# Beginning the second attention inside the local layers' last steps, and preparing batch 1 of the first attention beside the first maxima

## Chip, cores and metric

One core of a Trainium2 chip runs the whole program. The time is the device time of one execution in microseconds (us); lower is better. The engines are PE (matrix products), DVE (vector), ACT (scalar, activation functions), POOL (general, slower elementwise work) and SP (it issues most transfers). PSUM is the accumulator memory that PE writes, SBUF the working memory.

## The reference

The program is a chain of four blocks on `x` of 2 batches x 1024 tokens x 128 features, all in float32. Each block is followed by the sum with its own input and a layer norm.

```python
x = _layernorm(x + _L0_attn_ref(x, ...))   # 16 heads of 8, softmax over the keys, all 1024 keys
x = _layernorm(x + _L0_ffn_ref(x, ...))    # 2 local layers: windowed attention (window 64, 8 heads
                                           # of 64, rotary, l2 norm), then a gated GELU feed-forward
x = _layernorm(x + _L1_attn_ref(x, ...))   # causal attention, 2 query heads of 128, one key/value head
x = _layernorm(x + _L1_ffn_ref(x, ...))    # 8 experts, 2 chosen for each token
```

The first and the third are called first and second attention below.

## The kernel before

The order of the instructions is written out by hand. Every stage is a loop over steps, a function such as `project(n)` issues its instructions on several engines when it is called, and each engine runs its own in the order of the calls. Dictionaries (`also`, `early`, `late`, ...) hold further calls for certain steps: `at(late, 35, f)` means that `f` is called at the end of step 35. `late` comes last in a step.

**First attention** (`first_attention`, L136). It works in 16 units `m` (batch, group of four heads, half of the queries), units 0 to 7 for batch 0, 8 to 15 for batch 1. A unit takes 16 steps. In each step PE makes two score tiles of 128 x 512 (`max_score`, L226) whose maxima DVE takes (L232), and, `LATE` = 21 steps later, two transposed score tiles (`exp_score`, L258) that ACT exponentiates (L263) and PE multiplies with the values (L270). So steps 0 to 20 have only score tiles and maxima. At the end of each unit DVE combines its maxima (`max_row`, L236), PE turns the row, and ACT copies it out of PSUM (`max_shift`, L245). All PSUM tiles of this stage come from one ring of 8 (`ring`). Before the loop batch 0 is prepared: `prepare_x` transposes `x` (L88) and copies it to SBUF (L174), `project` makes keys and queries (L180, copies L182 and L184), `prepare_values` makes the values (L209, copy L213). Batch 1 is prepared by the same functions inside the loop: the six calls in `prepares` at steps 84, 86, ... 94, `prepare_values` at steps 132 and 134. Unit 8, at step 128, is the first that needs them; the transfers that spread its keys and queries over the partitions are issued at step 108.

**Local layers** (`local_layers`, L562). 32 tiles of 128 tokens go through a pipeline in steps 2 to 37; tile `n` is projected in step `n` and leaves in step `n + 6` (`add_x`), so that the last steps hold fewer and fewer functions. After every four tiles a feed-forward block follows (`ff_shift`, `ff_stats`, `ff_norm`, `ff_turn`, three chunks of `ff_in` and `ff_gate`, `ff_out`, `ff_add`). Of the last two blocks, (layer 1, batch 0, half 1) starts in step 33 and ends in step 37; (1, 1, 1) can start only when tile 31 has left and is computed in the second attention. The PSUM tiles are `double` (1024 wide, three) and `single` (512 wide, two). `last_sum` adds the block's input and prepares its norm.

**Second attention** (`second_attention`, L952). 16 tiles go through steps 0 to 20 (`one`). In step `n` tile `n` is projected (`project`, L970) and rotated (`rotate`: two products on DVE L983, a copy of the values on ACT L987, two sums on POOL L989 and L990); in step `n + 1` it is transposed (`transpose_qk`: PE L88, ACT L998 and L1001); in step `n + 2` come `scores` (L1012) and `exps` (DVE L1025 and L1026, ACT L1027). Its input comes from `head(b, hf)`: four transposes and an ACT copy (L963) for half a batch. Heads (0,0) and (1,0) are made before step 0. The last feed-forward block (1,1,1) is interleaved with steps 0 to 5, the norm of half (0,1) stands in step 1 and the norm of half (1,1) in step 6. `scores` and `ff_in` share the two `double` tiles of this stage's own PSUM pool `psc`.

The expert stage follows from step 16 on. Its loads, lookups and scatters are not touched.

Of the kernel before, what the change touches and what calls it, by code (L numbers as in the profile page):

```python
# [7 lines left out]
F32 = mybir.dt.float32  # L8
# [4 lines left out]
P = 128  # L13
B = 2
T = 1024
D = 128
# [31 lines left out]
def transformer_kernel(ctx: ExitStack, tc: tile.TileContext, a, out):  # L48
# [87 lines left out]
    def first_attention(pool, pool2, poolf, brief, psm, loads, experts, ws, tab, begin):  # L136
# [27 lines left out]
        def prepare_x(b, hf):  # L164
            if hf == 0:
                xTs[b] = pool2.tile([P, T], F32, tag="xT", name=f"xT{b}", bufs=1)
                zs[b] = poolf.tile([P, 8, D], F32, tag="z", name=f"z{b}", bufs=1)
                alls[b] = [
                    brief.tile([P, T], F32, tag=f"all{n}", name=f"all{n}{b}") for n in range(2)
                ]  # L170
            ps = ring("ps_xT")
            transpose_tiles(ps, lambda i: x[b, hf][:, i, :], 4)
            part = xTs[b][:, hf * 512 : (hf + 1) * 512]
            (nc.vector.tensor_copy if hf else nc.scalar.copy)(part, ps)  # L174

        def project(b, hf, n):

            ps = ring("ps_qk")
            part = slice(hf * 512, (hf + 1) * 512)
            nc.tensor.matmul(ps, wa[:, n, :], xTs[b][:, part], start=True, stop=True)  # L180
            if n == 0:
                nc.scalar.activation(alls[b][n][:, part], ps, AF.Copy, scale=8.0 ** -0.5)  # L182
            else:
                nc.vector.tensor_copy(alls[b][n][:, part], ps)  # L184

        def spread_k(u):

# [17 lines left out]
        def prepare_values(b, hf):  # L205
            ps = ring("ps_v")
            for i in range(4):
                t = hf * 4 + i
                nc.tensor.matmul(  # L209
                    ps[:, i * P : (i + 1) * P], xTs[b][:, t * P : (t + 1) * P], wa[:, 2, :],  # L210
                    start=True, stop=True,
                )
            nc.vector.tensor_copy(  # L213
                vps[b][:, hf * 4 : hf * 4 + 4, :, 0:8].rearrange("p t h d -> p (t h) d"),
                ps.rearrange("p (n d) -> p n d", d=8),
            )
# [123 lines left out]
        def at(step, f, *args):  # L340
            also.setdefault(step, []).append((f, args))
# [3 lines left out]
        for u in range(1, UNITS // 2):  # L345
            at(32 * u - 20, spread_q, u, 0, nc.sync)
            at(32 * u - 20, spread_k, u)
            at(32 * u - 20, spread_q, u, 1, nc.sync)
            for hf in range(2):
                at(32 * u - 4 + 2 * hf, keep_q, 2 * u + hf)  # L350
        for i, (f, *args) in enumerate(prepares):
            at(16 * 8 - 44 + 2 * i, f, 1, *args)
        for hf in range(2):
            at(16 * 8 + 4 + 2 * hf, prepare_values, 1, hf)
        for m in range(UNITS):
            at(16 * m + 15, max_row, m)
            at(16 * m + 16, max_shift, m)
# [204 lines left out]
    def local_layers(ws, tab):  # L562
# [282 lines left out]
            x_at[layer, b, hf] = x[b, hf]  # L845
            head(layer, b, hf)

        def steps(p, p2, ps, finish):
            nonlocal pool, pool2, psl
            pool, pool2, psl = p, p2, ps  # L850

# [59 lines left out]
            at(turns, 6, head, 0, 0, 1)  # L911
            at(turns, 10, head, 0, 1, 1)

            def run(f, n, *args):
                if 0 <= n < N:
                    f(n, *args)
# [32 lines left out]

    def second_attention(pool, pool2, poolf, single, double, route, wc, woc, cs, ws, left):  # L952
        N = 16
        tiles = [(b, t) for t in range(8) for b in range(B)]
        kTs = {b: pool.tile([P, T], F32, name=f"kTc{b}") for b in range(B)}
        vs = {b: pool.tile([P, 8, D], F32, name=f"vc{b}") for b in range(B)}
        xTs, ys, st = {}, {}, [{} for _ in range(N)]

        def head(b, hf):
            ps = single("ps_xTc")  # L960
            transpose_tiles(ps, lambda i: x[b, hf][:, i, :], NT)
            xTs[b, hf] = pool2.tile([P, 512], F32, tag="xTc", name="xTc", bufs=4)
            nc.scalar.copy(xTs[b, hf], ps)  # L963
            ys[b, hf] = pool2.tile([P, NT, D], F32, tag="yc", name=f"yc{b}{hf}", bufs=4)

        def project(n):
# [7 lines left out]
        def rotate(n):  # L974
            b, t = tiles[n]
            s = st[n]
            ps = s.pop("ps")

            q4 = ps[:, :384].rearrange("p (n d) -> p n d", d=64)
            t1 = pool2.tile([P, 3, 2, 64], F32, tag="t1c", name="t1c", bufs=2)  # L980
            t2 = pool2.tile([P, 3, 2, 64], F32, tag="t2c", name="t2c", bufs=2)
# [6 lines left out]
            rot = s["rot"] = pool2.tile([P, 3, 2, 64], F32, tag="rotc", name="rotc", bufs=2)  # L988
            nc.gpsimd.tensor_sub(rot[:, :, 0, :], t1[:, :, 0, :], t2[:, :, 1, :])  # L989
            nc.gpsimd.tensor_add(rot[:, :, 1, :], t1[:, :, 1, :], t2[:, :, 0, :])  # L990

        def transpose_qk(n):
            b, t = tiles[n]
            s = st[n]
            ps = single("ps_rotc")
            transpose_tiles(ps, lambda k: s["rot"][:, k].rearrange("p s d -> p (s d)"), 3)
            s["qT"] = pool2.tile([P, 2, P], F32, tag="qTc", name="qTc", bufs=3)
# [88 lines left out]
        def group(f, g, *args):  # L1086
            if 0 <= g < SOON:
                f(g, *args)


        norm_before, x_in, x1s, lasts = left
        ff_shift, ff_stats, ff_norm, ff_turn, ff_in, ff_gate, ff_out, ff_add = feed_forward(
            poolf, single, double, ws, x1s, lasts, mbufs=2, gbufs=4
        )
        early, late, normed = {}, {}, {}

        def at(when, step, f, *args):
# [2 lines left out]
        def do(when, step):  # L1100
            for f, args in when.pop(step, ()):
                f(*args)

        def sum_up(b):
            normed[b] = last_sum(x_in, b, 1)

        block = (1, 1, 1)
        at(late, 0, ff_shift, *block)
        at(late, 0, ff_stats, *block)
        at(early, 1, norm_before)  # L1110
        at(early, 1, ff_norm, *block)
        at(late, 1, ff_turn, *block)
        at(late, 1, head, 0, 1)
        for c, step in enumerate((2, 2, 3)):
            at(late, step, ff_in, *block, c)
            at(early, step + 1, ff_gate, *block, c)
        at(late, 4, ff_out, *block)
        at(early, 5, ff_add, *block)
        at(late, 5, sum_up, 1)
        at(early, 6, lambda: normed[1]())  # L1120
        at(late, 6, head, 1, 1)
        at(late, 1, route.lay_out)

        for b in range(B):
            head(b, 0)

        def one(step, run_experts):

# [46 lines left out]
                group(route.choose, p // 2)  # L1175
            do(late, step)

        def rest(run_experts):
            for step in range(FF_STEPS, N + 5):
                one(step, run_experts)  # L1180

        FF_STEPS = 8
        for step in range(FF_STEPS):
            one(step, None)
        assert not early and not late
        return rest

# [422 lines left out]
    ordered = {mybir.EngineType.PE, mybir.EngineType.Activation, mybir.EngineType.DVE}  # L1610
    engines = ordered | {mybir.EngineType.Pool}
    begin, steps = local_layers(ws, tab)
    with tc.tile_pool(name="af", bufs=1) as pf:


        brief = tc.tile_pool(name="a0", bufs=1, side="right")
        first = tc.tile_pool(name="l0", reuse_waits="tile", bufs=1, side="right")
        pb = brief.__enter__()

        def at_first():  # L1620
            brief.__exit__(None, None, None)
            return first.__enter__()

        with (
            tc.tile_pool(name="a1", bufs=1) as p1, tc.tile_pool(name="a2", bufs=2) as p2,
# [6 lines left out]
        with (  # L1632
            tc.tile_pool(name="l1", reuse_waits="tile", bufs=1) as p1,
            tc.tile_pool(name="l2", reuse_waits="tile", bufs=1) as p2,
            tc.tile_pool(name="psl", reuse_waits="tile", bufs=1, space=bass.MemoryType.PSUM) as psl,
            tc.manual_schedule(engines=engines),
        ):
            left = steps(p1, p2, psl, finish)
        first.__exit__(None, None, None)
    wlocal.__exit__(None, None, None)  # L1640
    with (
        tc.tile_pool(name="c1", reuse_waits="tile", bufs=1) as p1,
# [9 lines left out]

        route = Route(p1, p2, single, gate, xs)
        with tc.tile_pool(name="cf", reuse_waits="tile", bufs=1) as pf:
            rest = second_attention(p1, p2, pf, single, double, route, wc, woc, cs, ws, left)
        with tc.tile_pool(name="ce", reuse_waits="tile", bufs=1) as pe:
            run_experts = experts(pe, p2, single, double, route, ew, xs, yr)
            rest(run_experts)
            run_experts(4)


def _constants():
# [88 lines left out]
```

## Time and profile before

| what | value |
|---|---|
| median of 3 runs | 1090.54 us (1090.28 to 1091.72) |
| the profiled execution | 1090.38 us |
| its span, first to last instruction | 1088.6 us |
| busy: PE, DVE, ACT, POOL | 994.9, 802.0, 743.9, 569.3 us |
| granted PE clock, mean | 0.963 |
| first maxima (L226) to last exponent scores (L258) | 12.9 to 437.0 us |
| local layers up to the last `ff_out` (L528) | to about 830 us |
| second attention, first `project` to last `project` (L970) | 831.2 to 939.9 us |
| expert products (L1462) | 981.7 to 1062.8 us |

The span counts from the first to the last instruction; the execution's own time lies 1.8 us above it. A busy share is a mean over stages with different limits, so each stage is read from its own rows: a timeline row gives start, duration, engine, line, operation, output and inputs, count, and in brackets how long the engine had been idle and what ended that. For PE a count is of hardware passes, two for each float32 product.

### The profile page before, as it was taken

Reading aid. Unit: us, or ns where it says so; the run is one execution under the profiler, and the core shown is the slowest. Engines: PE = TensorE matmul, PEld = TensorE weight load, DVE = VectorE, ACT = ScalarE, POOL = GpSimd, SP = SyncE. Lnnn points to the kernel's source line nnn. Section 1 sums busy time; section 2 is a strip of 40 time slices with the busy share of each in tenths; the row PEclk is TensorE's granted clock in tenths of the full one; section 3 lists DMA queues with packets and bytes.
Section 4 is the critical chain, followed back from the end, with each engine's and each line's share of the span. In section 5 each row is a group of like instructions: output and inputs, shape, how many; then the busy total and the mean of one; then the engine's idle time right before and its main releaser. Section 6 shows DMA issues by size and latency. Waiting matters only on the chain. (4 is left out here: it accounts for less than half of the span.)

```text
span 1088.6 us, 21891 instructions
## 1 busy us (share of the span) xinstructions
PE 994.9 (91%) x8091; PEld 589.4 (54%) x8091; DVE 802.0 (74%) x1681; ACT 743.9 (68%) x1503; POOL 569.3 (52%) x625
## 2 busy tenths in 40 slices
PE   8999999999999999779889999999787799999991
PEld 4533333333333332356666657676564466689891
DVE  6988878888898886868969678696754387757443
ACT  1488878888888887568878788797763555444442
POOL 4134333434543433678978686786732135408753
PEclk9799999999999999989999999999898899999996
DMA  3111523122220200200101001010000000146883
GB/s 91 33 38 50 147 60 87 42 59 59 60 55 13 79 2 1 74 21 21 31 21 26 21 17 31 21 31 21 16 2 1 0 1 23 42 158 206 307 302 125
DMA packets 57210, 65.09 MB, mean 60 GB/s; under 512 B 9076, under 2 KB 43424, under 8 KB 57104
## 3 DMA queue, kind: packets, MB, share of 16 engines
q1 hardware_dynamic: 53472, 57.40, 17.9%
q0 software_dynamic: 2272, 4.92, 1.3%
q8 instruction: 64, 1.05, 0.4%
q10 hardware_dynamic: 1360, 1.38, 0.4%
q14 instruction: 42, 0.34, 0.1%
HBM read 37.98 MB, written 19.67 MB: 53 GB/s over the span
## 5 line engine op out<-in xcount | busy, mean ns | idle before, releaser
L232 DVE TENSOR_REDUCE mx<-s_max 128x1 f32<-128x512 f32 x512 | 318.2, 684 | 57.1 <-PE s_max L226 52.3
L263 ACT ACTIVATE pr<-s_exp 128x512 f32<-128x512 f32 x512 | 265.6, 602 | 71.1 <-PE s_max L226 58.7
L226 PE MATMUL s_max<-kTb,qm 32*128 32x512 f32 x1024 | 262.9, 642 | 0.5 <-DMA qm<-all 0.5
L282 POOL TENSOR_TENSOR av<-av,avp 128x512 f32<-128x512 f32 x101 | 128.0, 1267 | 245.7 <-ACT avp L281 226.6
L258 PE MATMUL s_exp<-q,kTb 32*128 32x512 f32 x1024 | 253.1, 616 | 0.0
L258 PEld LDWEIGHTS s_exp<-q,kTb 32*128 32x128 f32 x1024 | 101.2, 184 | 88.1 <-DVE mx L232 66.8
L270 PE MATMUL av<-pr,vp 128*32 128x512 f32 x1024 | 137.2, 605 | 0.7 <-ACT pr L263 0.7
L226 PEld LDWEIGHTS s_max<-kTb,qm 32*128 32x128 f32 x1024 | 113.6, 190 | 36.1 <-ACT pr L263 13.5
L755 ACT ACTIVATE pm<-pm,nb,rn 128x128 f32<-128x128 f32 x256 | 105.5, 490 | 0.1
L657 POOL TENSOR_TENSOR t<-raw,tab 128x512 f32<-128x512 f32 x64 | 87.1, 1381 | 19.4 <-DVE raw L625 10.8
L690 POOL TENSOR_TENSOR rn<-rn,neghalf 128x16 f32<-128x16 f32 x32 | 94.0, 2937 | 2.7
L649 DVE TENSOR_TENSOR t<-raw,tab 128x1024 f32<-128x1024 f32 x32 | 40.8, 1273 | 54.7 <-ACT raw L642 54.5
L270 PEld LDWEIGHTS av<-pr,vp 128*32 128x32 f32 x1024 | 20.5, 108 | 98.4 <-ACT pr L263 94.5
L636 PE MATMUL ps_qk<-wqkv,hT 128*128 128x512 f32 x120 | 58.8, 613 | 3.0 <-DVE o L788 2.5
L281 ACT COPY avp<-av 128x512 f32<-128x512 f32 x101 | 60.0, 594 | 1.8 <-PE av L270 0.6
L499 PE MATMUL ps_w<-hnT,w 128*128 128x512 f32 (+1 forms) x96 | 48.3, 635 | 13.1 <-DVE mt L517 9.8
L642 ACT COPY raw<-ps_qk 128x512 f32<-128x512 f32 x60 | 32.2, 589 | 38.1 <-PE ps_qk L636 37.4
L689 POOL TENSOR_SCALAR rn<-rn 128x16 f32<-128x16 f32 x32 | 31.1, 970 | 46.1 <-DVE rn L688 45.6
L1467 ACT ACTIVATE gj<-ps_fc 128x512 f32<-128x512 f32 x39 | 23.3, 597 | 41.2 <-PE ps_fc L1462 39.9
L1482 POOL DMA_INDIRECT yr<-yj,to x39 | 37.4, 958 | 23.1 <-DVE yj L1478 19.3
L688 DVE TENSOR_REDUCE rn<-sq 128x16 f32<-128x1024 f32 x32 | 38.6, 1208 | 9.5 <-ACT sq L664 9.4
L731 PEld LDWEIGHTS ps_sim<-kT,qT 64*64 64x64 f32 x1024 | 28.3, 135 | 31.9 <-issue 15.1
(230 smaller groups left out, 2012.1 us busy)
## 6 DMA issues: line engine op xcount, KB each, us to landing
wj<-ew SPq DMA_DIRECT2D x39, 512.0 KB
xs<-zero SPq DMA_DIRECT2D x8, 1152.0 KB
vh<-vb SPq DMA_DIRECT2D x60, 130.0 KB
xj<-xs SPq DMA_DIRECT2D x39, 72.0 KB
tab<-in_tab SPq DMA_DIRECT2D x2, 1024.0 KB
ew<-in_proj_w SPq DMA_DIRECT2D x8, 256.0 KB
ew<-in_fc_w SPq DMA_DIRECT2D x1, 2048.0 KB
wqkv<-in_wqkv SPq DMA_DIRECT2D x2, 768.0 KB
```

Of the source, the lines that this page charges most:

```text
L226: nc.tensor.matmul(s, q[32 * head : 32 * head + 32, qt * P : (qt + 1) * P], k[32 * head : 32 * head + 32, kh * 512 : (kh + 1) * 512], star ...
L232: return lambda: nc.vector.reduce_max(mx[:, head, qt, kh : kh + 1], s, axis=AX.X)
L258: nc.tensor.matmul(s, k[32 * head : 32 * head + 32, kt * P : (kt + 1) * P], q[32 * head : 32 * head + 32, :], start=True, stop=True,)
L263: return lambda: nc.scalar.activation(pr[:, head, :], s, AF.Exp)
L270: nc.tensor.matmul(ps[32 * h : 32 * h + 32, :], vps[m // 8][:, kt, 4 * g + h, :], pr[:, h, :], start=True, stop=True,)
L281: nc.scalar.copy(part, ps)
L282: nc.gpsimd.tensor_add(avs[m], avs[m], part)
L499: nc.tensor.matmul(ps[:m, n * 512 : (n + 1) * 512], w["w1"][:, n * HID + c0 : n * HID + c0 + m], f["hnT"], start=True, stop=True,)
L636: nc.tensor.matmul(ps[:, k * 512 : (k + 1) * 512], s["hT"], w["wqkv"][:, k * 512 : (k + 1) * 512], start=True, stop=True,)
L657: nc.gpsimd.tensor_mul(s["t2"][:, :, :, lo : lo + 32], raw4[:, :, :, hi : hi + 32], tabls[layer][:, t, 1, :, lo : lo + 32].unsqueeze(2).to ...
L690: nc.gpsimd.tensor_tensor(rn, rn, neghalf.to_broadcast([P, 16]), ALU.pow)
L755: nc.scalar.activation(s["pm"][:, k, :], s["pm"][:, k, :], AF.Exp, scale=s["rn"][:, head : head + 1], bias=s["nb"][:, k : k + 1],)
```

## The change

The change has two independent parts.

**Batch 1 of the first attention.** The six calls of `prepares` move from steps 84 to 94 to steps 1, 3, ... 11, and the two calls of `prepare_values` from 132 and 134 to 13 and 17. All their copies out of PSUM go to ACT for batch 1 (before, one of the two of `prepare_x`, both of the keys and both of the values were DVE's). The tiles `all0` and `all1` that hold queries and keys get a second buffer, so that batch 1 need not wait for batch 0's to be read.

**Second attention.** Heads (0,0) and (1,0), both of `project(0)`, `rotate(0)` and `project(1)`, `rotate(1)`, and `transpose_qk(0)` are called at the end of the local layers' steps 35, 36 and 37. They use the local layers' `double` PSUM tiles (their first 512 columns) and a new SBUF pool `c0` that takes the place of the pool `l0`. The second attention's loop then starts at step 2. The feed-forward block (1,1,1) and what hangs on it stand one step later than before: `ff_shift` and `ff_stats` ahead of step 2, `ff_norm` and `ff_turn` in step 2, `ff_in` in steps 3, 3 and 4, `ff_out` in 5, `ff_add` and the sum in 6, the norm and head (1,1) in 7.

```diff
-                    brief.tile([P, T], F32, tag=f"all{n}", name=f"all{n}{b}") for n in range(2)
+                    brief.tile([P, T], F32, tag=f"all{n}", name=f"all{n}{b}", bufs=2) for n in range(2)
...
-            (nc.vector.tensor_copy if hf else nc.scalar.copy)(part, ps)
+            (nc.vector.tensor_copy if hf and b == 0 else nc.scalar.copy)(part, ps)
...
-                nc.vector.tensor_copy(alls[b][n][:, part], ps)
+                (nc.scalar.copy if b else nc.vector.tensor_copy)(alls[b][n][:, part], ps)
...
-            nc.vector.tensor_copy(
+            (nc.scalar.copy if b else nc.vector.tensor_copy)(
                 vps[b][:, hf * 4 : hf * 4 + 4, :, 0:8].rearrange("p t h d -> p (t h) d"),
...
         for i, (f, *args) in enumerate(prepares):
-            at(16 * 8 - 44 + 2 * i, f, 1, *args)
+            at(1 + 2 * i, f, 1, *args)
         for hf in range(2):
-            at(16 * 8 + 4 + 2 * hf, prepare_values, 1, hf)
+            at(13 + 4 * hf, prepare_values, 1, hf)
...
+            for step, f, *args in after(double):
+                at(late, step, f, *args)
...
-        block = (1, 1, 1)
-        at(late, 0, ff_shift, *block)
-        at(late, 0, ff_stats, *block)
-        at(early, 1, norm_before)
-        at(early, 1, ff_norm, *block)
-        at(late, 1, ff_turn, *block)
-        at(late, 1, head, 0, 1)
-        for c, step in enumerate((2, 2, 3)):
-            at(late, step, ff_in, *block, c)
-            at(early, step + 1, ff_gate, *block, c)
-        at(late, 4, ff_out, *block)
-        at(early, 5, ff_add, *block)
-        at(late, 5, sum_up, 1)
-        at(early, 6, lambda: normed[1]())
-        at(late, 6, head, 1, 1)
...
-        for b in range(B):
-            head(b, 0)
...
+        def begin(p0, bank):
...
+            def enter():
+                nonlocal pool0, single
+                pool0, single = p0(), bank
+                for b in range(B):
+                    kTs[b] = pool0.tile([P, T], F32, name=f"kTc{b}")
+                    vs[b] = pool0.tile([P, 8, D], F32, name=f"vc{b}")
+                for b in range(B):
+                    head(b, 0)
+
+            def tile(n):
+                project(n)
+                rotate(n)
+
+            return [(35, enter), (36, tile, 0), (37, tile, 1), (37, transpose_qk, 0)]
...
+            block = (1, 1, 1)
+            ff_shift(*block)
+            ff_stats(*block)
+            at(early, 2, norm_before)
+            at(early, 2, ff_norm, *block)
+            at(late, 2, ff_turn, *block)
+            at(late, 2, head_too, 0, 1)
+            for c, step in enumerate((3, 3, 4)):
+                at(late, step, ff_in, *block, c)
+                at(early, step + 1, ff_gate, *block, c)
+            at(late, 5, ff_out, *block)
+            at(early, 6, ff_add, *block)
+            at(late, 6, sum_up, 1)
+            at(early, 7, lambda: normed[1]())
+            at(late, 7, head_too, 1, 1)
...
+            for step in range(2, FF_STEPS):
+                one(step, None)
...
+            left = steps(
+                p1, p2, psl, finish,
+                lambda double: begin2(at_second, lambda name: double(name)[:, :512]),
+            )
```

More of the change, by code (lines that the diff above doesn't have):

```diff
@@ L846, in next_head, with steps @@
             head(layer, b, hf)
-        def steps(p, p2, ps, finish):
+        def steps(p, p2, ps, finish, after):
             nonlocal pool, pool2, psl
@@ L946, in local_layers, with second_attention @@
         return begin, steps
-    def second_attention(pool, pool2, poolf, single, double, route, wc, woc, cs, ws, left):
+    def second_attention(wc, woc, cs, ws):
+        pool0 = pool2 = single = double = route = None
         N = 16
         tiles = [(b, t) for t in range(8) for b in range(B)]
-        kTs = {b: pool.tile([P, T], F32, name=f"kTc{b}") for b in range(B)}
-        vs = {b: pool.tile([P, 8, D], F32, name=f"vc{b}") for b in range(B)}
-        xTs, ys, st = {}, {}, [{} for _ in range(N)]
+        kTs, vs, xTs, ys, st = {}, {}, {}, {}, [{} for _ in range(N)]
         def head(b, hf):
@@ L961, in head, with make_y @@
             transpose_tiles(ps, lambda i: x[b, hf][:, i, :], NT)
-            xTs[b, hf] = pool2.tile([P, 512], F32, tag="xTc", name="xTc", bufs=4)
+            xTs[b, hf] = pool0.tile([P, 512], F32, tag="xTc", name="xTc", bufs=4)
             nc.scalar.copy(xTs[b, hf], ps)
+        def make_y(b, hf):
             ys[b, hf] = pool2.tile([P, NT, D], F32, tag="yc", name=f"yc{b}{hf}", bufs=4)
@@ L979, in rotate @@
             q4 = ps[:, :384].rearrange("p (n d) -> p n d", d=64)
-            t1 = pool2.tile([P, 3, 2, 64], F32, tag="t1c", name="t1c", bufs=2)
-            t2 = pool2.tile([P, 3, 2, 64], F32, tag="t2c", name="t2c", bufs=2)
+            t1 = pool0.tile([P, 3, 2, 64], F32, tag="t1c", name="t1c", bufs=2)
+            t2 = pool0.tile([P, 3, 2, 64], F32, tag="t2c", name="t2c", bufs=2)
             for k, o in enumerate((t1, t2)):
@@ L987, in rotate @@
             nc.scalar.copy(vs[b][:, t, :], ps[:, 384:512])
-            rot = s["rot"] = pool2.tile([P, 3, 2, 64], F32, tag="rotc", name="rotc", bufs=2)
+            rot = s["rot"] = pool0.tile([P, 3, 2, 64], F32, tag="rotc", name="rotc", bufs=2)
             nc.gpsimd.tensor_sub(rot[:, :, 0, :], t1[:, :, 0, :], t2[:, :, 1, :])
@@ L996, in transpose_qk @@
             transpose_tiles(ps, lambda k: s["rot"][:, k].rearrange("p s d -> p (s d)"), 3)
-            s["qT"] = pool2.tile([P, 2, P], F32, tag="qTc", name="qTc", bufs=3)
+            s["qT"] = pool0.tile([P, 2, P], F32, tag="qTc", name="qTc", bufs=3)
             nc.scalar.activation(
@@ L1088, in group @@
                 f(g, *args)
[L1091 to L1094, printed above, removed]
         early, late, normed = {}, {}, {}
@@ L1102, in do @@
                 f(*args)
-        def sum_up(b):
-            normed[b] = last_sum(x_in, b, 1)
-        block = (1, 1, 1)
-        at(late, 0, ff_shift, *block)
-        at(late, 0, ff_stats, *block)
-        at(early, 1, norm_before)
-        at(early, 1, ff_norm, *block)
-        at(late, 1, ff_turn, *block)
-        at(late, 1, head, 0, 1)
-        for c, step in enumerate((2, 2, 3)):
-            at(late, step, ff_in, *block, c)
-            at(early, step + 1, ff_gate, *block, c)
-        at(late, 4, ff_out, *block)
-        at(early, 5, ff_add, *block)
-        at(late, 5, sum_up, 1)
-        at(early, 6, lambda: normed[1]())
-        at(late, 6, head, 1, 1)
-        at(late, 1, route.lay_out)
-        for b in range(B):
-            head(b, 0)
         def one(step, run_experts):
@@ L1176, in one @@
             do(late, step)
+        FF_STEPS = 8
         def rest(run_experts):
@@ L1180, in rest, with steps, sum_up, head_too @@
                 one(step, run_experts)
[L1182 to L1186, printed above, removed]
+        def begin(p0, bank):
+            nonlocal pool0, single
+            def enter():
+                nonlocal pool0, single
+                pool0, single = p0(), bank
[8 more added lines that the diff above has]
+            return [(35, enter), (36, tile, 0), (37, tile, 1), (37, transpose_qk, 0)]
+        def steps(p2, poolf, sgl, dbl, rt, left):
+            nonlocal pool2, single, double, route
+            pool2, single, double, route = p2, sgl, dbl, rt
+            norm_before, x_in, x1s, lasts = left
+            ff_shift, ff_stats, ff_norm, ff_turn, ff_in, ff_gate, ff_out, ff_add = feed_forward(
+                poolf, single, double, ws, x1s, lasts, mbufs=2, gbufs=4
+            )
+            def sum_up(b):
+                normed[b] = last_sum(x_in, b, 1)
+            def head_too(b, hf):
+                head(b, hf)
+                make_y(b, hf)
+            block = (1, 1, 1)
[13 more added lines that the diff above has]
+            at(late, 7, head_too, 1, 1)
+            at(late, 2, route.lay_out)
+            for b in range(B):
+                make_y(b, 0)
+            for step in range(2, FF_STEPS):
+                one(step, None)
+            assert not early and not late
+            return rest
+        return begin, steps
     class Route:
@@ L1612, in transformer_kernel @@
     begin, steps = local_layers(ws, tab)
+    begin2, steps2 = second_attention(wc, woc, cs, ws)
     with tc.tile_pool(name="af", bufs=1) as pf:
@@ L1617, in transformer_kernel @@
         first = tc.tile_pool(name="l0", reuse_waits="tile", bufs=1, side="right")
+        second = tc.tile_pool(name="c0", reuse_waits="tile", bufs=1, side="right")
         pb = brief.__enter__()
@@ L1622, in at_first, with at_second @@
             return first.__enter__()
+        def at_second():
+            first.__exit__(None, None, None)
+            return second.__enter__()
         with (
@@ L1637, in transformer_kernel @@
         ):
-            left = steps(p1, p2, psl, finish)
-        first.__exit__(None, None, None)
+            left = steps(
+                p1, p2, psl, finish,
+                lambda double: begin2(at_second, lambda name: double(name)[:, :512]),
+            )
     wlocal.__exit__(None, None, None)
@@ L1654, in transformer_kernel @@
         with tc.tile_pool(name="cf", reuse_waits="tile", bufs=1) as pf:
-            rest = second_attention(p1, p2, pf, single, double, route, wc, woc, cs, ws, left)
+            rest = steps2(p2, pf, single, double, route, left)
         with tc.tile_pool(name="ce", reuse_waits="tile", bufs=1) as pe:
@@ L1659, in transformer_kernel @@
             run_experts(4)
+    second.__exit__(None, None, None)
 def _constants():
```

## The prediction

> **What bounds the kernel now.** The stages run one after another, so I read, for each stage that the change touches, what paces it.
>
> The first view is ACT's timeline, cut to the copies of the row of maxima (L245): one for each unit of 16 steps, a metronome of the first attention.
>
> ```profile
> 131.45 0.25 ACT L245 COPY row<-ps_nm 16x128 f32<-16x128 f32 x1
> 161.23 0.25 ACT L245 COPY row<-ps_nm 16x128 f32<-16x128 f32 x1
> 185.64 0.25 ACT L245 COPY row<-ps_nm 16x128 f32<-16x128 f32 x1
> 210.05 0.25 ACT L245 COPY row<-ps_nm 16x128 f32<-16x128 f32 x1
> 236.67 0.25 ACT L245 COPY row<-ps_nm 16x128 f32<-16x128 f32 x1
> ```
>
> 161.23 to 185.64 and 185.64 to 210.05 are 24.41 us each, the bare unit. 131.45 to 161.23 is 29.78: this unit holds the six `prepares` of batch 1. 210.05 to 236.67 is 26.62: the two `prepare_values`.
>
> The second view is the timeline of DVE and ACT where only maxima are made.
>
> ```profile
> 16.94 18.03 DVE L232 TENSOR_REDUCE mx<-s_max 128x1 f32<-128x512 f32 x30 [0.95 <-PE s_max L226]
> ...
> 35.66 0.26 ACT L245 COPY row<-ps_nm 16x128 f32<-16x128 f32 x1 [21.15 <-PE ps_nm L243]
> ```
>
> DVE reduces without a gap, 0.60 us a tile; ACT has been idle for 21.15 us. DVE paces this stretch, and ACT is free.
>
> The third is the table by stretches (PE, PEld, DVE, ACT, POOL busy, then the granted PE clock).
>
> ```profile
> 18.00:20.00 2.00, 2.00 (x14) 1.09 (x7) 2.00 (x5) 0.00 (x0) 0.61 (x1) 0.81 0.14 25
> 20.00:22.00 2.00, 2.00 (x9) 1.01 (x8) 2.00 (x5) 0.00 (x0) 0.00 (x0) 1.00 0.27 38
> ...
> 28.00:30.00 2.00, 2.00 (x10) 1.69 (x8) 2.00 (x4) 0.00 (x0) 0.00 (x0) 0.50 0.00 0
> ...
> 836.00:840.00 4.00, 0.51 (x3) 0.26 (x3) 3.72 (x15) 0.71 (x3) 2.64 (x5) 0.74 0.01 2
> 840.00:844.00 4.00, 3.52 (x10) 2.23 (x11) 1.20 (x4) 1.36 (x2) 1.26 (x13) 0.50 0.02 4
> ```
>
> A lightly loaded PE falls to half clock: at 28 us, harmless under DVE's pace, and at 840 us, after a hole.
>
> The last is PE's timeline at the seam between local layers and second attention.
>
> ```profile
> 819.70 5.32 PE L499 MATMUL ps_w<-hnT,w 128*128 128x512 f32 x12
> ...
> 827.25 2.84 PE L528 MATMUL ps_w<-w,mt 128*128 128x128 f32 x24
> 829.93 1.04 PE L88 MATMUL ps_xTc<-cst,x 128*128 128x128 f32 x8
> 831.21 1.12 PE L970 MATMUL ps_qkv<-wc,xTc 128*128 128x512 f32 x2 [0.24 <-ACT xTc L963]
> 832.17 0.59 PE L464 MATMUL ps_sh<-xl,cst 128*128 128x256 f32 x2
> ...
> 840.49 1.25 PE L88 MATMUL ps_hn<-cst,h 128*128 128x128 f32 x4 [3.98 <-DVE h L118]
> ...
> 842.38 1.91 PE L970 MATMUL ps_qkv<-wc,xTc 128*128 128x512 f32 x2
> ...
> 847.97 5.40 PE L499 MATMUL ps_w<-hnT,w 128*128 128x512 f32 x8 [2.61 <-ACT pc L1027]
> ```
>
> Here nothing is full: a chain of short dependent steps over all engines sets the end. From the last `ff_out` (829.93) to step 2's `project` (842.38) 12.45 us pass, the steps 0 and 1 that the change moves.
>
> **Part A, batch 1 prepared early.** Removed: 29.78 - 24.41 = 5.37 and 26.62 - 24.41 = 2.21, together 7.58 us. These are lengthenings of a strictly periodic unit, so they already count all that the eight calls cost there.
>
> Added, in steps 1 to 17. DVE: nothing; its five copies go to ACT. ACT: eight copies of about 0.6 us (a 128x512 copy in L281 takes 0.59), about 5 us inside the 21.15 idle. If that cover were gone they would cost the 5 us. SP and POOL: no transfer is added, and the spreading for unit 8 keeps step 108. PE: two transpose groups of 0.66, four `project` of 1.12, two value groups of 1.16, one beside four score tiles every 2.4 us of DVE (4 x 0.60). Four score tiles cost PE at most 1.02 us at full clock (a bare unit has 24 groups of four: 24.41 / 24). So 1.02 + 1.16 = 2.18 fits under 2.4. At half clock it does not: 2 x (1.02 + 1.12) = 4.28, 1.88 too long for each `project`, 1.96 for each value group, 0.96 for each transpose group, 13.4 us in all. These are the bounds, 0 and 13.4; below nothing is excluded, because DVE keeps the same reduces in this stretch.
>
> I take 0.8, close to the lower end: in the row of 20 to 22 us the clock stands at 1.00 with less work for PE than it will have. Only the first transposes fall into DVE's start, where it still waits for PE (the 0.95 before 16.94), at half clock: 0.66 to 1.32 us, part of it under the two reduces that are ready. Part A: -7.58 + 0.8 = -6.8.
>
> **Part B, the seam.** I followed the changed program's order and its waits, with the durations above and their neighbours' (times without part A's shift).
>
> The local layers' end becomes longer. After the first `ff_in` (819.70 + 1.77 = 821.5) PE makes 8 transposes (1.04), and the second `ff_in` now waits for ACT's copy of the first head, which has its PSUM tile: gelu ends at 822.31, the copy (0.59) at 822.9. The third ends at 826.6 (before 825.0). Then gelu 0.68 and gate 0.75, while PE does the output of tile 31 and `project(0)` (1.02) until 830.0; `ff_out` runs 829.9 to 832.7, 2.6 us late.
>
> Then comes a wait that the source does not show. `ff_shift` is the first user of the new PSUM pool, over the tile in which `project(1)` lay, and so waits until ACT has copied that tile's values, which waits for DVE's products, which stand behind the sum: `ff_add` 0.69 (833.5), POOL sum 1.27 (834.8), statistics 1.15 (835.9), products 1.03 (837.0), copy 0.27 (837.3). `ff_shift` stood at 832.17; now 837.3, 5.1 late. Queued behind it on PE: `project(2)`, the turning of tile 1, scores 0.
>
> On from there: shift 1.26, copy 0.4, statistics 1.15, products of tile 2 1.05, the two norms 1.38 and 1.65 put DVE at 844.2; masks and maxima of scores 0 (1.2), then two exponents: scores 0 done at 846.1 (before 848.2). `project(2)` starts near 838.4, 4.0 earlier than 842.38. The last block's first `ff_in` now stands behind the exponents of tile 1, another 3.7 us on (turning 0.49, scores 0.49, masks and maxima 1.2, exponents 0.6, ACT's copies in between 0.9): about 849.8 against 847.97, 1.8 late. From that `ff_in` to the second step after the one with `ff_out` the order is the old one with tile numbers one higher. Before, that stretch led from 847.97 to step 5 at 867.91; so step 6 starts at 869.7. Before, step 6 started at 871.28: 1.6 us gained. The sum and norm of (1,1), one step later too, are work that moved, not work added. Bounds: -4.0 (all that `project(2)` gains stays) and, if the last block paces everything to its end, 5.1 late instead of 1.8: 873.0 for step 6, +1.7. I take -1.6, by the chain worked out.
>
> Behind the seam every stage keeps its order, so the shift reaches the end.
>
> Here a rule of the Trainium skill speaks against the change. Row first: after the hole of 3.98 us before 840.49 the clock was 0.50. The page "TensorE: Matmul & The Clock Gate", section "HAM oscillation — how this bites in real kernels", warns of PE idle gaps over about 3.4 us, after which the clock falls back to half. My order has a hole from 833.9 to 837.3 and loses the old one, so by the rule the cost would be the old one again and the sum the same; by the row, 3.4 us may just miss the drop, and the sum would be up to 1.9 us better (the first two `ff_in` at 0.44 a pass instead of 5.40 for eight).
>
> **Sum.** 1090.4 (this execution; the median lies 0.16 above) - 6.8 - 1.6 = 1082.0.
>
> **Rivals.**
> - The seam pays less than nothing: the last block paces it, +1.7, so 1090.4 - 6.8 + 1.7 = 1085.3. For: `ff_shift` 5.1 late. Against: 1.8 us of lag remain where the exponents catch up. Chance 0.19.
> - The seam keeps the whole lead of `project(2)`: 1090.4 - 6.8 - 4.0 = 1079.6. For: one old hole with half clock goes. Against: the new one. Chance 0.16.
> - Part A is given back in its new place: half clock in the four `project` steps alone, 4 x 1.88 = 7.5, leaves 1090.4 - 0.1 - 1.6 = 1088.7. Chance 0.05.
> - Slower: half clock through all eight pieces, 13.4 us in steps 1 to 17. PE, not DVE, then paces the maxima: 1090.4 - 7.58 + 13.4 - 1.6 = 1094.6. It decides from 9.2 us, six pieces of the eight. For: the rows from 26 to 38 us at 0.50. Against: these rows have PE at 1.02 us of full-clock work in 2.4, the new ones twice that. Chance 0.04.
> - The forecast: 0.56.
>
> **How the numbers follow.** A measurement of this kernel tells 0.2%, 2.2 us, from no change. The forecast and the first two rivals are faster (0.91); the third lies within 0.2% (0.05); the fourth is slower (0.04). Range: upwards to the first rival with 2 us instead of 0.8 lost in part A, 1090.4 - 7.58 + 2.0 + 1.7 = 1086.5; downwards to the second with nothing lost there and the two `ff_in` at full clock (eight passes at 0.44, as at 819.70, instead of 5.40: 1.9 us), 1090.4 - 7.58 - 4.0 - 1.9 = 1076.9. What is left out is the last two rivals, 0.09, and what I have not seen.
>
> **What would show it.** Right: the two long units at 24.41, DVE without a gap from about 17 to 35 us, ACT's eight copies there; `ff_out` about 2.6 us later against the step before it, `ff_shift` waiting on ACT's copy L987, `project(2)` about 4 us earlier after `ff_out`'s old place. Wrong: maxima spaced wider than 0.60 us while the clock is 0.50, or a unit that stays long without the calls; then A's sum falls. `ff_shift` before the sum's statistics would refute the hidden wait.

## The result

The changed kernel takes 1084.63 us (median of 8 executions, 1083.42 to 1086.69), the kernel before 1090.81 (8 executions beside them). The ratio is 0.9953 with a 95% interval of 0.9943 to 0.9963: 5.1 us faster, 4.0 to 6.2 (the two medians themselves lie 6.2 us apart). The forecast was 1082.0, 8.4 below the profiled execution of the kernel before. The changed kernel's profiled execution took 1084.36 us, its span is 1082.6, its mean clock 0.971.

First ACT's timeline of the changed kernel, the copies of the row of maxima (start, duration, engine, line, operation):

```profile
37.64 0.25 ACT L245 COPY row<-ps_nm 16x128 f32<-16x128 f32 x1 [4.23 <-PE ps_nm L243]
60.15 0.25 ACT L245 COPY row<-ps_nm 16x128 f32<-16x128 f32 x1
...
133.37 0.25 ACT L245 COPY row<-ps_nm 16x128 f32<-16x128 f32 x1
157.78 0.25 ACT L245 COPY row<-ps_nm 16x128 f32<-16x128 f32 x1
182.18 0.25 ACT L245 COPY row<-ps_nm 16x128 f32<-16x128 f32 x1
206.59 0.25 ACT L245 COPY row<-ps_nm 16x128 f32<-16x128 f32 x1
231.00 0.25 ACT L245 COPY row<-ps_nm 16x128 f32<-16x128 f32 x1
```

The two long units are gone: 133.37 to 157.78 and 206.59 to 231.00 are 24.41 us each. From the first copy to the 16th (406.31, before 412.80) the stage lasts 368.67 us where it lasted 377.14: 8.5 us less, of which 0.7 lie in a later unit (308.24 to 332.68, before 314.04 to 339.17) that nothing was taken from: there two norm products on DVE (L118) took 1.60 us at 320.10 before and 0.59 at 314.31 now. But the first copy comes 1.98 us later. DVE's timeline and the table by stretches (busy PE, PEld, DVE, ACT, POOL, then the granted PE clock) show why:

```profile
15.99 1.35 DVE L232 TENSOR_REDUCE mx<-s_max 128x1 f32<-128x512 f32 x2 [0.37 <-PE s_max L226]
19.69 2.48 DVE L232 TENSOR_REDUCE mx<-s_max 128x1 f32<-128x512 f32 x4 [2.35 <-PE s_max L226]
22.61 14.44 DVE L232 TENSOR_REDUCE mx<-s_max 128x1 f32<-128x512 f32 x24 [0.43 <-PE s_max L226]
```

```profile
16.00:18.00 2.00, 2.00 (x9) 1.13 (x12) 1.34 (x2) 0.31 (x1) 0.00 (x0) 0.50 0.14 25
18.00:20.00 2.00, 2.00 (x10) 0.50 (x7) 0.31 (x1) 0.28 (x1) 0.61 (x1) 0.50 0.14 25
20.00:22.00 2.00, 2.00 (x12) 0.84 (x10) 2.00 (x4) 0.58 (x1) 0.00 (x0) 0.50 0.28 41
22.00:24.00 2.00, 2.00 (x10) 0.61 (x10) 1.57 (x4) 0.32 (x1) 0.00 (x0) 0.93 0.27 41
```

DVE waits 2.35 us for PE, which runs the first preparing calls and the score tiles at clock 0.50 until 22 us.

Now PE's timeline at the seam, and further down in step 7:

```profile
812.74 1.88 PE L500 MATMUL ps_w<-hnT,w 128*128 128x512 f32 x4
...
822.68 2.84 PE L529 MATMUL ps_w<-w,mt 128*128 128x128 f32 x24
825.35 1.02 PE L976 MATMUL ps_qkv<-wc,xTc 128*128 128x512 f32 x2
...
830.08 0.70 PE L465 MATMUL ps_sh<-xl,cst 128*128 128x256 f32 x2 [3.38 <-ACT vc L993]
...
831.11 1.88 PE L976 MATMUL ps_qkv<-wc,xTc 128*128 128x512 f32 x2
...
841.15 3.70 PE L500 MATMUL ps_w<-hnT,w 128*128 128x512 f32 x8 [1.05 <-ACT pc L1033]
...
864.35 1.02 PE L976 MATMUL ps_qkv<-wc,xTc 128*128 128x512 f32 x2
...
873.07 0.66 PE L1279 MATMUL ps_xr<-cst,xe 128*128 128x128 f32 x2 [5.42 <-DVE xe L1269]
...
877.68 1.70 PE L976 MATMUL ps_qkv<-wc,xTc 128*128 128x512 f32 x2
```

and the same step 7 in the kernel before:

```profile
877.32 1.03 PE L970 MATMUL ps_qkv<-wc,xTc 128*128 128x512 f32 x2
...
882.11 0.30 PE L1245 MATMUL ps_xr<-cst,xe 128*128 128x128 f32 x1
...
884.41 1.10 PE L970 MATMUL ps_qkv<-wc,xTc 128*128 128x512 f32 x2
```

PE stands idle for 3.38 us until ACT's copy of the values lets `ff_shift` start, as forecast. 864.35 is `project(7)`, before at 877.32: 12.97 us earlier. The local layers' `ff_in` of step 35 came 6.96 earlier (812.74, before 819.70), so the seam is 6.0 us ahead here. Then a wait that was in no step of the prediction: PE stands 5.42 us before `ps_xr`, the routing's turning of the first pair of tiles. 877.68 is `project(8)`, before at 884.41: 6.73 earlier, 0.2 behind the shift. In one step the whole lead is gone.

What DVE and POOL do there, from their timelines:

```profile
862.19 0.68 DVE L538 TENSOR_TENSOR xf<-ps_w,xl 128x512 f32<-128x512 f32 x1
...
865.69 0.30 DVE L1260 BATCH_NORM_AGGREGATE r_mv<-r_st 128x2 f32<-128x6 f32 x2
868.38 0.88 DVE L99 BATCH_NORM_STATS2 ln_st<-yl 128x6 f32<-128x128 f32 x4 [2.39 <-POOL yl L545]
...
871.00 1.67 DVE L118 TENSOR_SCALAR x<-yl,ln_mv,ln_rs 128x128 f32<-128x128 f32 x4 [0.56 <-POOL ln_rs L106]
872.59 0.59 DVE L1269 TENSOR_SCALAR xe<-yc,r_mv,r_rs 128x128 f32<-128x128 f32 x2
```

```profile
862.99 0.59 POOL L996 TENSOR_TENSOR rotc<-t1c,t2c 128x192 f32<-128x192 f32 x1
866.08 0.23 POOL L1261 TENSOR_SCALAR r_rs<-r_mv 128x2 f32<-128x2 f32 x1 [2.50 <-DVE r_mv L1260]
866.39 0.72 POOL L1262 TENSOR_TENSOR r_rs<-r_rs,neghalf 128x2 f32<-128x2 f32 x1
867.09 1.26 POOL L545 TENSOR_TENSOR yl<-xf,x 128x512 f32<-128x512 f32 x1
```

POOL in the kernel before, where the sum runs long ahead of `r_rs`:

```profile
871.34 1.27 POOL L544 TENSOR_TENSOR yl<-xf,x 128x512 f32<-128x512 f32 x1
...
880.61 0.71 POOL L1228 TENSOR_TENSOR r_rs<-r_rs,neghalf 128x2 f32<-128x2 f32 x1
```

The feed-forward's sum `yl` needs `xf`, done at 862.9, and POOL has finished tile 6's rotation at 863.6. But the sum stands in POOL's queue behind the routing's `r_rs`, which waits for DVE's `r_mv`; so it starts at 867.09. DVE waits 2.39 us for it, makes its statistics, the products of tile 7 and the norm (1.67), and only then `xe`, whose inputs have been there since 867.1. PE's outputs (L1059), the transposes of head (1,1) and `project(8)` are queued behind `ps_xr`. The routing takes its statistics (`route.stats`) in even steps and its norm and turning in odd ones. Before, the sum stood in odd step 5 and the norm in even step 6, out of its way. One step later, the sum falls in the even step 6 and the norm in the odd step 7.

### The profile page after: what moved, and what is told of

Its sections match the earlier page's. It is cut to its first block, busy times and chain, and to the rows that moved or that the text cites. A ratio compares the mean times of both kernels' runs of the same rounds, so it can differ in the third digit from the quotient of the medians.

```text
span 1082.6 us, 21876 instructions
## 1 busy us (share of the span) xinstructions
PE 986.8 (91%) x8091; PEld 582.2 (54%) x8091; DVE 796.5 (74%) x1676; ACT 746.4 (69%) x1508; POOL 569.5 (53%) x625
## 4 chain that ended last, share of the span: by engine, by line
PE 61%; DVE 18%; POOL 8%; ACT 7%; issue 4%; DMA 2%; ACTq 0%; POOLq 0%; SPq 0%; DVEq 0%
PE s_exp L258 13%; PE av L270 12%; PE s_max L226 10%; PE ps_qk L637 4%; PE ps_w L500 3%; POOL yr L1516 2%; PE ps_sc L1018 2%; PE ps_oc L1059 2%; ACT pm L756 2%; DVE pm L740 2%; DVE nb L745 2%; ACT raw L643 2%; DVE t L650 2%; PE ps_w L529 1%; DVE rn L689 1%
## 5 line engine op out<-in xcount | busy, mean ns | idle before, releaser
L226 PE MATMUL s_max<-kTb,qm 32*128 32x512 f32 x1024 | 255.6, 624 | 0.4 <-DMA qm<-all 0.3
L226 PEld LDWEIGHTS s_max<-kTb,qm 32*128 32x128 f32 x1024 | 104.4, 185 | 34.2 <-ACT pr L263 15.5
L658 POOL TENSOR_TENSOR t<-raw,tab 128x512 f32<-128x512 f32 x64 | 86.1, 1365 | 19.4 <-DVE raw L626 10.8
L500 PE MATMUL ps_w<-hnT,w 128*128 128x512 f32 (+1 forms) x96 | 45.5, 602 | 12.8 <-DVE mt L518 9.6
```

Source lines behind the costliest of these rows:

```text
L226: nc.tensor.matmul(s, q[32 * head : 32 * head + 32, qt * P : (qt + 1) * P], k[32 * head : 32 * head + 32, kh * 512 : (kh + 1) * 512], star ...
L500: nc.tensor.matmul(ps[:m, n * 512 : (n + 1) * 512], w["w1"][:, n * HID + c0 : n * HID + c0 + m], f["hnT"], start=True, stop=True,)
L658: nc.gpsimd.tensor_mul(s["t2"][:, :, :, lo : lo + 32], raw4[:, :, :, hi : hi + 32], tabls[layer][:, t, 1, :, lo : lo + 32].unsqueeze(2).to ...
```

## The experiments

Differences in us are the ratio to the kernel before times its median beside it, with the 95% interval. The stretch is a reading of each profile that leaves the start out: from the local layers' `ff_in` of step 35 to `project(10)`, which holds the seam and steps 0 to 9.

| kernel | median us | against before, us | stretch, us |
|---|---|---|---|
| before | 1089.5 to 1090.8 | | 76.29 |
| changed | 1084.63 | -5.1 (-6.2 to -4.0) | 77.12 |
| after_again | 1084.71 | -5.1 (-6.9 to -3.3) | 77.56 |
| a_alone | 1082.32 | -7.6 (-8.9 to -6.2) | 76.31 |
| b_alone | 1092.31 | +2.3 (+1.3 to +3.3) | 77.33 |
| before_sum_even | 1095.33 | +5.2 (+3.8 to +6.6) | 81.04 |
| sum_odd | 1080.08 | -10.8 (-12.5 to -9.0) | 73.43 |
| shift_free | 1084.26 | -5.7 (-7.4 to -4.0) | 74.85 |
| prep_late | 1083.71 | -6.3 (-8.2 to -4.4) | 77.15 |
| free_odd | 1079.17 | -11.1 (-13.0 to -9.2) | 70.81 |
| odd_late | 1077.94 | -11.3 (-13.1 to -9.5) | 72.99 |
| all_three | 1075.27 | -14.7 (-16.8 to -12.6) | 70.64 |

**Each part by itself.** `a_alone` is the kernel before with the diff's hunks in `first_attention` alone, `b_alone` the changed kernel with these undone.

> Only part A: batch 1 is prepared in steps 1 to 17, the seam stays as it was. Theory (the seam's lead is given back in step 7, so the whole gain is part A's): about 6.5 us below the kernel before, near 1084.0, that is within 1 us of the changed kernel; first score rows spaced 24.41 us throughout, the first of them about 2 us late. Rival (the prediction's sum, in which the seam brings 1.6 us that stay): the whole change is 6.0 us better than before, so part A alone would show 4.4, near 1086.2.

> Only part B: the second attention begun within the local layers, batch 1 prepared at the old steps. Theory: the lead of project(7), 6.0 us against project(7) before, is lost in steps 7 and 8, where PE waits over 5 us for DVE's xe; the time is that of the kernel before, or up to 0.8 us more: 1090.5 to 1091.6. Rival (the prediction): 1.6 us less, 1089.2. Second rival (the lead stays): 4 to 6 us less, 1085 to 1087.

Part A alone is 7.6 us faster than before, and faster than the whole change. Part B alone is 2.3 us slower. Both differences lie beyond the theory's figures, by 1.1 and 1.5 us, and on the side away from the prediction. In `b_alone` PE waits 5.43 us for `xe`, as in the changed kernel. Its stretch, 77.33 us against 76.29 before, shows 1.0 of the 2.3 us; the rest lies outside the seam and its place is not shown. So the whole gain is part A's, and part B takes some of it back.

**The sum moved off the even step.**

```diff
-            at(late, 6, sum_up, 1)
-            at(early, 7, lambda: normed[1]())
-            at(late, 7, head_too, 1, 1)
+            at(late, 7, sum_up, 1)
+            at(early, 8, lambda: normed[1]())
+            at(late, 8, head_too, 1, 1)
...
-        FF_STEPS = 8
+        FF_STEPS = 9
```

> The changed kernel with the sum and norm of half (1,1) one more step later (sum at the end of step 7, norm and head in step 8), so that the sum again falls in an odd step, as before the change, and not in an even one with the routing's statistics. Theory: the wait of 5.42 us for xe in step 7 falls below 1 us, project(8) comes 5 to 6 us earlier, step 8 pays 0.5 to 1.5 us for the norm, and about 4.5 us of it reach the end: near 1080.0. Rival (the hole is the price of pair 0's routing after a shorter step 6, whatever stands beside it): the hole stays, time within 1 us of the changed kernel, 1084.6. Second rival (the lead is lost again further on, in the expert stage): project(8) early, last products not, 1084.

The time agrees with the theory, 1080.08 against 1080.0. PE's timeline of `sum_odd`:

```profile
864.75 1.02 PE L976 MATMUL ps_qkv<-wc,xTc 128*128 128x512 f32 x2
...
868.32 0.30 PE L1279 MATMUL ps_xr<-cst,xe 128*128 128x128 f32 x1 [0.27 <-DVE xe L1269]
...
870.61 1.10 PE L976 MATMUL ps_qkv<-wc,xTc 128*128 128x512 f32 x2
...
878.91 1.12 PE L976 MATMUL ps_qkv<-wc,xTc 128*128 128x512 f32 x2 [2.31 <-ACT xTc L967]
```

The wait is 0.27 us instead of 5.42, and step 7 lasts 5.86 us instead of 13.33. Step 8 pays: `project(9)` now waits 2.31 us for head (1,1), because DVE makes the norm in that step (0.5 to 1.5 us had been expected). What is left, 3.7 us of the stretch, reaches the end: the time is 4.6 us below the changed kernel's by the medians, 5.7 by the ratios.

**The same collision in the old kernel.** Only the three `at` lines of the sum, norm and head are moved, one step later, in the kernel before.

> The kernel before with nothing changed but the sum and norm of half (1,1) one step later (sum at the end of step 6, norm and head in step 7). Theory: the same collision makes the same hole in the old kernel: a wait of about 5 us for xe in step 7; step 6 is about 1 us shorter without the norm; so 4 to 5 us slower than before, near 1095. Rival (the collision needs the rest of part B): within 1 us of before, 1090.5.

Slower by 5.2 us. PE's and POOL's timelines of `before_sum_even`:

```profile
875.29 1.02 PE L970 MATMUL ps_qkv<-wc,xTc 128*128 128x512 f32 x2
...
883.93 0.66 PE L1245 MATMUL ps_xr<-cst,xe 128*128 128x128 f32 x2 [5.34 <-DVE xe L1235]
...
888.54 1.04 PE L970 MATMUL ps_qkv<-wc,xTc 128*128 128x512 f32 x2
```

```profile
877.24 0.73 POOL L1228 TENSOR_TENSOR r_rs<-r_rs,neghalf 128x2 f32<-128x2 f32 x1
877.95 1.26 POOL L544 TENSOR_TENSOR yl<-xf,x 128x512 f32<-128x512 f32 x1
```

The same wait, with the same sum behind the same `r_rs`, without any other part of the change. This settles the cause: the even step, not the seam. The edit moves sum and norm together; how much of the wait comes from the sum behind `r_rs` on POOL and how much from the norm ahead of `xe` on DVE is not separated.

**The hidden wait of `ff_shift`.** Its PSUM place is moved: the new pool's 1024-wide tiles lie first, and tile 0's transposed queries and keys take a 512-wide tile of the local layers' pool.

```diff
-            for step, f, *args in after(double):
+            for step, f, *args in after(double, single):
...
-                lambda double: begin2(at_second, lambda name: double(name)[:, :512]),
+                lambda double, single: begin2(
+                    at_second, lambda name: single(name) if name == "ps_rotc" else double(name)[:, :512]
+                ),
...
+        double("ps_none")
         route = Route(p1, p2, single, gate, xs)
```

> The changed kernel with other PSUM places at the seam: the transposed keys and queries of tile 0 use a 512-wide tile of the local layers' pool, and the new pool's 1024-wide tiles lie first, so that ff_shift is no longer over project(1)'s tile. Theory: PE's wait of 3.38 us ahead of ff_shift goes, but DVE copies its result only behind the products of tile 1, for which it stood idle 1.64 us: so the norm and the last block come about 1.6 us earlier, and 1.0 to 1.6 us of it reach the end: near 1083.0. Rival (ff_shift's lateness of 4.9 us paces the block): 3.4 us or more earlier, near 1080.5. Second rival (the hole in step 7 takes it too): no change, 1084.4.

The wait ahead of `ff_shift` is gone; PE now stands idle for 2.85 us after `project(2)`. PE's and DVE's timelines of `shift_free`:

```profile
826.04 1.02 PE L976 MATMUL ps_qkv<-wc,xTc 128*128 128x512 f32 x2
...
827.23 0.60 PE L465 MATMUL ps_sh<-xl,cst 128*128 128x256 f32 x2
...
832.08 0.90 PE L88 MATMUL ps_rotc<-cst,rotc 128*128 128x128 f32 x3 [2.85 <-POOL rotc L996]
```

```profile
829.83 0.55 DVE L989 TENSOR_TENSOR t2c<-ps_qkv,cs 128x384 f32<-128x384 f32 x1
830.30 0.42 DVE L480 COPY h<-ps_sh 128x256 f32<-128x256 f32 x1
```

Counted from `project(0)` (822.51 here, 821.82 in the changed kernel) `ff_shift` stands 3.54 us earlier, but DVE's copy of its result only 1.70: it now follows the products of tile 1 without a gap. The stretch is 2.3 us shorter than the changed kernel's. The time, 0.45 us below `after_again`, does not resolve this. In the profiled execution step 10 and the expert products, which the edit does not touch, took 1.7 and 0.7 us longer than in the profile of the changed kernel. The two pairs of kernels below, with and without this edit, tell more.

**Batch 1 prepared four steps later.**

```diff
-            at(1 + 2 * i, f, 1, *args)
+            at(5 + 2 * i, f, 1, *args)
...
-            at(13 + 4 * hf, prepare_values, 1, hf)
+            at(17 + 2 * hf, prepare_values, 1, hf)
```

> The changed kernel with the eight preparing calls of batch 1 four steps later: steps 5 to 15 and 17, 19. Theory: the first of them then fall where the clock is back at 1.00 and DVE has tiles in store; DVE's 32 first reduces take 20.2 to 21.0 us whatever the clock at 16 to 20 us, and the time is 0.5 to 2 us less than the changed kernel's: near 1083.2. Rival (PE's extra work costs the same anywhere in this stretch): no change, 1084.4.

> The changed kernel once more, to stand beside the three below on one chip and to see how its start differs from one execution to the next. Theory (the cost of part A at the start follows the clock that PE is granted from 14 to 22 us): 1083 to 1085; from DVE's first reduce of scores to the end of the 32nd about 21.0 us where the profiled start is at full clock, 22.4 to 23.4 where half clock falls into it. Rival (the cost is fixed, 2 us): 23.4 whatever the clock.

DVE's first 32 reduces, from the start of the first to the end of the last, against the clock: in the old order 21.0, 20.6 and 20.2 us (before, `before_sum_even`, `b_alone`). In the changed order 23.4, 22.4 and 22.4 (changed, `a_alone`, `shift_free`) where the clock fell to between 0.50 and 0.62 in the rows from 16 to 20 us, but 21.0 in `sum_odd` and `after_again`, where these rows are at 1.00. With the calls four steps later 20.2, although this execution had the low clock. DVE's timeline and the table of `prep_late`:

```profile
16.32 18.03 DVE L232 TENSOR_REDUCE mx<-s_max 128x1 f32<-128x512 f32 x30 [0.18 <-PE s_max L226]
```

```profile
16.00:18.00 2.00, 2.00 (x16) 1.46 (x10) 1.82 (x4) 0.00 (x0) 0.15 (x1) 0.55 0.14 25
18.00:20.00 2.00, 2.00 (x8) 0.46 (x3) 2.00 (x5) 0.00 (x0) 0.61 (x1) 0.59 0.14 25
```

and the table of `after_again`, the changed kernel itself in another execution:

```profile
16.00:18.00 2.00, 2.00 (x15) 0.74 (x13) 1.29 (x2) 0.59 (x1) 0.00 (x0) 1.00 0.14 25
18.00:20.00 2.00, 2.00 (x17) 1.07 (x14) 1.92 (x4) 0.59 (x1) 0.62 (x1) 1.00 0.14 25
```

So the cost of part A at the start is not fixed: by the reduces 0 to 0.8 us at full clock, and 1.4 to 3.2 in these three executions with the low clock. The first 32 reduces do not show all of it: in `a_alone` and `shift_free` the second unit is long as well (24.1 us, 22.5 in the changed kernel). From the first reduce to the 16th copy of the row of maxima the old order took 398.0 to 398.8 us, the changed order 390.2 at full clock (`sum_odd`, `after_again`) and 392.0 to 393.3 with the low clock (changed, `a_alone`, `shift_free`, `free_odd`), and the kernels with the later calls 389.4 to 389.5 (`prep_late`, `odd_late`, `all_three`). So the low clock cost 1.8 to 3.1 us, and the later calls save 0.7 even at full clock. No run sets the clock; cost and low clock came together in all six profiles of this order. In the medians the 1.0 us between `prep_late` and `after_again` lies within their intervals.

**Together, and two at a time.** `all_three` has the three edits above, `free_odd` lacks the later preparing, `odd_late` lacks the PSUM places.

> The changed kernel with all three edits: sum and norm of half (1,1) one more step later, ff_shift off project(1)'s tile, batch 1 prepared four steps later. Theory: the gains stand in different stages and add up: 4.5 + 1.3 + 1.0, near 1077.5 (against 1084.4 of the changed kernel). Rival (step 8 with the norm, where PE waited 2.31 us for xTc, takes the seam's 1.3 back): near 1079.

> all_three without the later preparing: sum and norm one more step later, and ff_shift off project(1)'s tile. Theory: from project(0) to the first expert product about 147.0 us, as in all_three (sum_odd: 149.80, the changed kernel: 153.72); the first stage again by the clock at 16 to 22 us, 0.7 to 3.2 us longer than in all_three in some executions: near 1076.5. Rival (the PSUM places bring nothing, as the time of shift_free suggests): 149.8 us for that stretch, and a time near 1079.

> all_three without the other PSUM places: sum and norm one more step later, batch 1 prepared four steps later. Theory: DVE's 32 first reduces take 20.3 us, as in all_three; from project(0) to the first expert product 149 to 150 us, as in sum_odd: near 1077.5. Rival (the PSUM places bring nothing): the time of all_three, 1075.3.

`all_three` is the fastest kernel of the study, 14.7 us below the kernel before and 9.4 below the changed one by their medians; more than the 7 us expected. By the medians the three edits bring 6.0 us one at a time, by the ratios 7.5 (9.6 together); where the rest comes from is not shown. The stretch puts a figure on the PSUM places: 73.43 to 70.81 without the later preparing, 72.99 to 70.64 with it, 2.6 and 2.4 us; by the ratios the same pairs differ by 0.3 and 3.4. From `project(0)` to the first expert product `free_odd` took 147.15 us and `odd_late` 148.07, against 147.0 and 149 to 150 expected; over this longer stretch the PSUM places bring 2.7 and 1.1 us, because `odd_late` took 40.92 us from `project(15)` to the first expert product, which no edit touches, and the other three 42.19. `odd_late` is 0.4 us from the time of its theory. `free_odd` was slower than its theory by 2.7 us, at its rival's figure, although its stretch is the theory's; its profiled start had the low clock (32 reduces in 21.9 us, clock 0.77 and 0.50; 392.0 us to the 16th copy against 389.5 in `all_three`).

## Why the prediction was right in sign and 3 us too good

- **Removed in part A, 7.58 us.** Right, and 0.9 short: 8.5 us left the stage. The 0.7 in a later unit was not foreseen. It goes with the pair of norm products on DVE, long in all three profiles with the old order and short in all nine with the new; why stays open.
- **Added at the start, 0.8 us.** The value fits only at full clock. In the profiled execution it was 2.4 us by the reduces (23.4 against 21.0). The argument from the row at 20 to 22 us, clock 1.00, was too thin: that clock came back later in this execution, and half clock covered more than the first transposes, up to 22 us. The wait came where DVE has no stock of tiles, as said, but longer than the 0.66 to 1.32 us. Part A was forecast at -6.8 and is -7.6 by itself: right within its interval.
- **The seam up to step 6.** `ff_out` 2.4 us late (2.6 forecast), `ff_shift` 4.9 late through the hidden wait (5.1), `project(2)` 4.3 early (4.0): all right. The last block's first `ff_in` was 0.1 late instead of 1.8, and ran 3.70 us instead of 5.40 since the half clock was over by then. So the lead at `project(6)` was 4.2 us where the chain gave 1.6; the other five profiles with the same order up to there gave 2.7 to 4.2.
- **The step that failed** is the pair of sentences "The sum and norm of (1,1), one step later too, are work that moved, not work added" and "Behind the seam every stage keeps its order, so the shift reaches the end". As work they moved. But the routing does not move with them: its statistics stay in step 6 and its norm in step 7. The pairs of neighbours in POOL's and DVE's queues changed, and step 7 took 13.33 us instead of 7.09. `before_sum_even` shows this loss alone, `sum_odd` shows it avoided. The seam was forecast at -1.6 and is +2.3 by itself; that is 3.9 of the miss, of which part A gave 0.8 back. By the stretch the seam is +1.0, which makes its miss 2.6. Either way its sign was wrong, and the sign of the whole came out right through part A alone.
- **The rivals.** 1085.3 is nearest in its figure and wrong in its reason: the last block did not pace the seam. 1079.6, the lead kept, is what `sum_odd` brings.
- **The clock rule.** The hole of 3.38 us before `ff_shift` was followed by a row of clock 0.66 (830 to 834 us), and `project(2)` took 1.88 us instead of 1.02; the hole of 5.42 us by a row of 0.50 (874 to 878 us). These two holes agree with the Trainium skill, "TensorE: Matmul & The Clock Gate", section "HAM oscillation — how this bites in real kernels", which warns of gaps over about 3.4 us. "May just miss the drop" was wrong. But shorter holes were followed by the low clock too: the 2.85 us of `shift_free` by 0.50 from 832 to 838 us, and 1.76 us in `after_again` by 0.63 and 0.52 from 836 to 840 us. So no run here shows a limit at 3.4 us, and the measurement decides. The `ff_in` still gained the 1.7 us, because the low clock was spent on short products before it: from 838 to 846 us the clock was 1.00. "A lightly loaded PE falls to half clock" holds only at times: the prediction's own row of 20 to 22 us has the same score tiles as the row at 28 us and stands at 1.00.

## What to carry to other kernels

When a hand-ordered step is moved, the work that stays is half of the question: list, for each engine's queue, who stands next to whom in the new step, above all where another function runs in every second step. A lead is safe only behind the last place where two schedules meet. Extra work in front of an engine's first stock of tiles should be priced at the low clock too.

## What the runs showed of the hardware

The clock falls without a hole as well, and not in every execution. The changed kernel has 0.50 from 16 to 22 us in one execution and 1.00 in the other, with PE shown as busy throughout these rows in both. In step 10 the same eight score products (L1018) took 2.41 us in the changed kernel and 3.75 in `after_again` (clock 1.00 and 1.00 against 0.64 and 0.51 from 894 to 898 us), and `project(11)` followed `project(10)` after 9.05 and 10.73 us. Such steps of 1 to 2 us in stages that no edit touches are a likely reason why gains of single edits of about 1 us and less stayed undecided in the medians here, while a stretch read in the profile told them apart.
